# Two mixture-of-experts layers on one core: the routed experts' loop staged by quads of slot tiles instead of pairs

## The chip, the cores and the metric

The kernel runs on one core of a Trainium2 chip. A core has five engines, each with an instruction stream of its own that is worked off in order: TensorE (PE in the profile, its weight loads PEld), VectorE (DVE), ScalarE (ACT), GpSimd (POOL) and SyncE (SP). They meet through semaphores only. PE reads SBUF and writes PSUM (eight banks of 512 float32 a partition); DVE and ACT take results out of PSUM. DMAs are issued from the streams of SP and ACT, and indirect ones (a row index for each row) from POOL's.

The metric is the device time of one execution in microseconds; the time of a kernel is the median of its runs.

## What is computed

The input is x of 4 x 1024 tokens with 256 channels, all float32. Two layers, each `x = x + s * silu(ffn(xn))` with `xn` the layer norm of x and `s` a mixer of `xn`: in layer 0 a gated linear recurrence over the 1024 steps, in layer 1 an attention over cosines. The part that matters here is the ffn, a mixture of 16 experts of which each token takes 4, chosen by group-limited top-k. In layer 0:

```python
g = jnp.einsum('th,eih->tei', x, gate_proj)
u = jnp.einsum('th,eih->tei', x, up_proj)
act = jax.nn.silu(g) * u
expert_out = jnp.einsum('tei,ehi->teh', act, down_proj)
y = jnp.einsum('teh,te->th', expert_out, combine)
```

Layer 1 has the same form with a shared expert of 512 hidden channels added. An expert's hidden width is 128 in layer 0 and 64 in layer 1.

## The kernel before

Tokens are sorted by expert. A router gives each of a token's four choices a *slot*; the token's row is scattered to `rows_in` in DRAM by indirect DMA on POOL (line 587). Slots are cut into tiles of 128 rows, every tile belongs to one expert, and four tiles make a quad. Each layer has two groups of tokens and 160 tiles in all, which is 80 pairs or 40 quads. `experts` (from line 592) is a generator that both layers use; `w_sb` holds all experts' weights, and a register that PE loads from `of_tile` (line 480, eight tiles at a time) says where a tile's expert begins.

For a pair of tiles the generator has four steps:

- `turn` (lines 635 and 639): the rows `xs` of a quad come by one DMA (line 626, three quads ahead, on SP in layer 0 and mostly on ACT in layer 1); PE transposes two tiles by two halves of 128 channels into a bank `tp`, and ACT copies it to `xT`.
- `hidden` (line 647, then 473, 474 and 658): PE multiplies `xT` by gate and up weights into a bank `gu` (64 x 2 or 128 x 2 columns a tile, so in layer 1 half the bank is left free); ACT makes tanh, DVE two steps, and the result is `h`.
- `turn_hidden` (lines 664 and 666): PE transposes the two tiles of `h` into a bank `tp`, ACT copies them to `hT`. In layer 1 a transposed tile has 64 partitions.
- `down` (line 672): PE multiplies `hT` by the down weights into a bank `acc`. The first pair of a quad is copied to `o` by DVE (line 690), the second by ACT (line 684); then the quad is stored, in layer 0 by one DMA on ACT's queue (line 723), in layer 1 by four indirect DMAs on POOL (line 1212).

The steps are pipelined by pairs. Round j of the loop issues `turn` of pair j+2, `hidden` of j+1, `turn_hidden` of j and `down` of j-1, with a `yield` after each. Two copies of a bank and four of `xT`/`h` (tag `act`) and `sg`/`hT` (tag `sg`) are there.

The yields set what is mixed in. `run` counts a planned clock on by 0.81 (layer 0) or 0.64 us (layer 1) a yield, and lets other generators, `Beside`, issue their pieces when they are due: in layer 0 the last recurrence, the combine of finished groups (gathers on POOL, line 730) and layer 1's routing; in layer 1 preparation of the last batch for the attention (line 1013), and the final combine, `gated1` (line 1250). The tile framework then orders each engine's stream by its own estimate; what is listed below as a program's order is the built one. After layer 0's experts come attention and shared expert for three batches beside the combine, then the dispatch of layer 1 (128 scatters), layer 1's experts, and the last batch's shared expert and attention.

Of the kernel before, what the change touches and what calls it, by code (L numbers as in the profile page):

```python
# [9 lines left out]
F32 = mybir.dt.float32  # L10
# [6 lines left out]
P = 128  # L17
B, S, D = 4, 1024, 256
# [5 lines left out]
XB, GB, QB, OB = 8, 4, 3, 3  # L24
# [6 lines left out]
QUAD = 4  # L31
# [32 lines left out]
def two_layer_kernel(  # L64
# [18 lines left out]
    nc = tc.nc  # L83
# [3 lines left out]
    work = ctx.enter_context(tc.tile_pool(name="work", bufs=2))  # L87
# [5 lines left out]
    def bank(tag, bufs):  # L93
        tag = side[0] if tag == "side" else tag
        return psum.tile([P, 512], F32, tag=tag, name=tag, bufs=bufs)
# [42 lines left out]
    ident = const.tile([P, P], F32, tag="ident", name="ident")  # L138
# [3 lines left out]
    for n in (G, E):  # L142
        m = const.tile([P, max(2 * NT, *(len(h) * NS for h in HALVES)), n], F32, tag=f"run{n}", name=f"run{n}")
# [43 lines left out]
    def latest(engine):  # L187
        return next(i for i in reversed(nc.cur_bb.bb.instructions) if i.engine == engine)
# [282 lines left out]
    def twice_silu(dst, t, v):  # L471

        nc.scalar.activation(t, v, AF.Tanh, scale=0.5)  # L473
        nc.vector.scalar_tensor_tensor(dst, t, 1.0, v, ALU.add, ALU.mult)  # L474

    def offset(table, engine, u, cache, most):

        if u not in cache:
            n = min(8, table.shape[1] - u)
            _, values = nc.values_load_multi_w_load_instructions(  # L480
                table[0:1, u : u + n],
                engines=[engine],
                min_val=0,
                max_val=most,
                skip_runtime_bounds_check_because="the kernel holds it to the last expert's",
            )
            for i, v in enumerate(values):
                cache[u + i] = v
        return cache[u]
# [14 lines left out]
    def by_quads(rows):  # L504

        return rows.rearrange("(n p i) d -> n p i d", p=P, i=QUAD)
# [94 lines left out]
    def experts(groups, of_tiles, w_sb, we, hid, store, target=None, begin=None, end=None):  # L601

        per = QUAD // 2
        quads = [(i, g, q) for i, g in enumerate(groups) for q in range(NSLOT[g] // QUAD)]
        n = len(quads) * per
        width = rows_in[groups[0]].shape[1]
        offsets, loaded, made, targets = [{} for _ in groups], {}, {}, {}  # L610

        def expert(t):
            i, _, q = quads[t // QUAD]
            return offset(of_tiles(i), mybir.EngineType.PE, q * QUAD + t % QUAD, offsets[i], (E - 1) * we)

        def load(at):
            if at >= len(quads):
                return
            _, g, q = quads[at]
            if q == 0 and begin:  # L620
                begin(g)
            xs = work.tile([P, QUAD, D + INFO], F32, tag="q", name="xs", bufs=QB)
            xs = xs.rearrange("p i d -> p (i d)")[:, 0 : QUAD * width].rearrange("p (i d) -> p i d", d=width)

            engine = nc.scalar if g >= G1 and at > 2 else nc.sync
            engine.dma_start(out=xs, in_=by_quads(rows_in[g])[q])
            loaded[at] = xs

        def turn(j):
            xs = loaded[j // per]  # L630
            tp = bank("tp", 2)
            for i in range(2):
                for kc in range(KC):
                    at = (i * KC + kc) * P
                    nc.tensor.transpose(  # L635
                        tp[:, at : at + P], xs[:, j % per * 2 + i, kc * P : (kc + 1) * P], ident
                    )
            xT = work.tile([P, 2, KC, P], F32, tag="act", name="xT", bufs=4)
            nc.scalar.copy(xT.rearrange("p i k t -> p (i k t)"), tp)  # L639
            return xT  # L640

        def hidden(j, xT):
            ps = bank("gu", 2)[:, 0 : 4 * hid]
            for i in range(2):
                off = expert(2 * j + i)
                for kc in range(KC):
                    nc.tensor.matmul(  # L647
                        ps[:, i * 2 * hid : (i + 1) * 2 * hid],
                        lhsT=xT[:, i, kc, :],
                        rhs=w_sb[:, bass.ds(off + kc * 2 * hid, 2 * hid)],  # L650
                        start=(kc == 0),
                        stop=(kc == KC - 1),
                    )
            gu = ps.rearrange("p (i w h) -> p i w h", i=2, w=2)
            sg = work.tile([P, 2, hid], F32, tag="sg", name="sg0", bufs=4)
            h = work.tile([P, 2, hid], F32, tag="act", name="h0", bufs=4)
            twice_silu(h, sg, gu[:, :, 0, :])
            nc.vector.tensor_tensor(h, h, gu[:, :, 1, :], ALU.mult)
            return h

        def turn_hidden(h):
            tp = bank("tp", 2)
            for i in range(2):
                nc.tensor.transpose(tp[0:hid, i * P : (i + 1) * P], h[:, i, :], ident)  # L664
            hT = work.tile([P, 2 * P], F32, tag="sg", name="hT0", bufs=4)
            nc.scalar.copy(hT[0:hid, :], tp[0:hid, 0 : 2 * P])  # L666
            return hT

        def down(j, hT):
            ps = bank("acc", 2)  # L670
            for i in range(2):
                nc.tensor.matmul(  # L672
                    ps[:, i * D : (i + 1) * D],
                    lhsT=hT[0:hid, i * P : (i + 1) * P],
                    rhs=w_sb[0:hid, bass.ds(expert(2 * j + i) + 4 * hid, D)],
                    start=True,
                    stop=True,
                )
            if j % per == 0:
                made[j // per] = work.tile([P, QUAD, D], F32, tag="o", name="o", bufs=OB)  # L680
            o = made[j // per]
            to = o[:, j % per * 2 : j % per * 2 + 2, :].rearrange("p i d -> p (i d)")
            if j % per == per - 1:
                nc.scalar.copy(to, ps)
                _, g, q = quads[j // per]
                store(g, q, made.pop(j // per), targets.pop(j // per, None))
                if end and q == NSLOT[g] // QUAD - 1:
                    end(g)
            else:
                nc.vector.tensor_copy(to, ps)  # L690

        xT, h, hT = {}, {}, {}
        load(0)
        load(1)
        load(2)
        yield
        for j in range(-2, n + 1):
            if j + 2 < n:
                at, last = divmod(j + 2, per)
                if last and target:  # L700

                    with tc.issue_after(latest(mybir.EngineType.DVE)):
                        targets[at] = target(quads[at][2], loaded[at])
                xT[j + 2] = turn(j + 2)
                if last:
                    loaded.pop(at)
                    load(at + 3)
            yield
            if 0 <= j + 1 < n:
                h[j + 1] = hidden(j + 1, xT.pop(j + 1))  # L710
            yield
            if 0 <= j < n:
                hT[j] = turn_hidden(h.pop(j))
            yield
            if 0 <= j - 1:
                down(j - 1, hT.pop(j - 1))
            yield

    def experts0():


        def store(g, q, o, _):
            nc.scalar.dma_start(out=by_quads(rows_out[g])[q], in_=o)

        return experts(range(G1), lambda i: routed[i][1], w0_sb, WE, P, store, end=stored.add)
# [460 lines left out]
    def experts1():  # L1186
# [35 lines left out]
        def end(g):  # L1222
            stored1[g - G1] = max(clock[0], pool_free[0]) + LANDING

        return experts(range(G1, 2 * G1), lambda i: placed1[i][2], we1_sb, WE1, P // 2, store, target, begin, end)

    def gated1(b):
# [250 lines left out]
```

## Time and profile before

| what | value |
|---|---|
| median of 4 runs (lowest, highest) | 1443.6 us (1440.87, 1448.89) |
| the profiled execution's own time | 1447.49 us |
| its span, first to last instruction | 1445.8 us |
| mean granted clock of TensorE | 0.861 of full |
| busy: PE, PEld, DVE, ACT, POOL | 1084.8, 796.0, 648.2, 461.6, 559.1 us |
| gates, line 647: 1280 matmul records | 248.0 us busy |
| down, line 672: 640 records | 188.2 us busy |
| row transposes, line 635: 640 | 105.4 us busy |
| transposes of `h`, line 664: 320 | 64.1 us busy |
| result stores, line 1212: 160 | 159.9 us busy |

A float32 matmul stands in the trace as two records, a transpose as one. Matmuls are pipelined: the duration of a record covers its way through the array, and the next starts earlier than it ends, so the cost of one in a stream is the step from start to start. `PEclk` is the share of full clock that PE was granted. "issue" as the end of an idle time means that the profile shows nothing the engine waited for.

### The profile page before, as it was taken

The page shows a single profiled execution, that of the slowest core. Times are in us where ns is not written, and L with a number is a line of the kernel's source. Part 1 is how long each engine was busy: PE and PEld are TensorE (multiplying, and loading weights), DVE is VectorE, ACT ScalarE, POOL GpSimd, SP SyncE. Part 2 cuts the span into 40 slices and gives each one's busy share as a digit, 9 for nine tenths or more (in the row PEclk, how much of TensorE's full clock was granted, in tenths as well). Part 3 has the DMA queues.
Part 4 walks back from the last instruction along what each step waited for, and adds up shares of the span by engine and source line. Part 5 has one row for each costly group of instructions (what it writes and reads, how often), then busy time and mean ns, then how long its engine had stood idle before and what let it go on. Part 6 is the DMA issues. An engine that isn't in the chain of part 4 may idle for free.

```text
span 1445.8 us, 16114 instructions
## 1 busy us (share of the span) xinstructions
PE 1084.8 (75%) x4928; PEld 796.0 (55%) x4928; DVE 648.2 (45%) x1928; ACT 461.6 (32%) x1028; POOL 559.1 (39%) x589
## 2 busy tenths in 40 slices
PE   6427671399938989938688934625999998999997
PEld 4214351288837778726356712314767676666566
DVE  4903930033227863125976714200235333567485
ACT  3503440144314544302222400001226443454322
POOL 0470377400254000254332775771004665566300
PEclk9756895599969999957889976857999999899999
DMA  9983254377958668765235624320113555896681
GB/s 347 415 325 88 88 160 158 120 210 218 263 169 289 196 168 228 288 163 168 81 108 184 209 104 152 132 104 37 73 66 130 174 169 185 286 318 228 200 271 56
DMA packets 118994, 264.81 MB, mean 183 GB/s; under 512 B 14208, under 2 KB 71680, under 8 KB 117632
## 3 DMA queue, kind: packets, MB, share of 16 engines
q1 hardware_dynamic: 78256, 138.79, 30.8%
q0 software_dynamic: 27264, 75.86, 15.5%
q10 hardware_dynamic: 13392, 49.14, 9.6%
q8 instruction: 43, 0.70, 0.2%
q14 instruction: 39, 0.32, 0.1%
HBM read 119.34 MB, written 144.39 MB: 182 GB/s over the span
## 4 chain that ended last, share of the span: by engine, by line
PE 55%; another core or an unknown queue 18%; DVE 16%; issue 6%; ACT 3%; DMA 1%; POOL 0%; ACTq 0%; DVEq 0%; POOLq 0%
PE gu L647 13%; PE acc L672 10%; PE tp L635 5%; PE acc L1098 5%; PE gu L1145 4%; PE tp L664 3%; PE acc L1161 3%; PE mm L1145 3%; PE mm L1066 2%; PE gu L1013 1%; DVE stats L197 1%; PE acc L301 1%; DVE hT L545 1%; PE mm L519 1%
## 5 line engine op out<-in xcount | busy, mean ns | idle before, releaser
L730 POOL DMA_INDIRECT r<-rows_out,row x128 | 128.4, 1003 | 368.8 <-issue 172.8
L647 PE MATMUL gu<-w_sb,xT 128*128 x1280 | 248.0, 338 | 4.0 <-issue 3.0
L1212 POOL DMA_INDIRECT results<-o,dest x160 | 159.9, 1000 | 213.4 <-DVE h L474 129.7
L647 PEld LDWEIGHTS gu<-w_sb,xT 128*128 128x128 f32 x1280 | 201.6, 199 | 20.0 <-issue 5.0
L672 PE MATMUL acc<-w_sb,hT 128*128 (+1 forms) x640 | 188.2, 411 | 8.0 <-ACT hT L666 8.0
L587 POOL DMA_INDIRECT rows_in<-x_half,row x128 | 132.1, 1032 | 137.1 <-issue 88.4
L474 DVE SCALAR_TENSOR_TENSOR h<-sg,gu 128x256 f32<-128x256 f32 (+1 forms) x160 | 56.1, 351 | 261.5 <-ACT sg L473 196.3
L1098 PE MATMUL acc<-val,es 128*128 128x256 f32 x512 | 132.6, 402 | 27.0 <-ACT es L1078 25.1
L587 POOL DMA_INDIRECT rows_in<-t_half,row x128 | 125.9, 984 | 39.4 <-issue 37.0
L635 PE MATMUL tp<-ident,xs 128*128 128x128 f32 x640 | 105.4, 289 | 41.8 <-ACT xT L639 21.6
L672 PEld LDWEIGHTS acc<-w_sb,hT 128*128 128x128 f32 (+1 forms) x640 | 111.6, 196 | 38.0 <-issue 16.8
L639 ACT COPY xT<-tp 128x512 f32<-128x512 f32 x160 | 93.8, 587 | 112.3 <-PE tp L635 49.8
L1098 PEld LDWEIGHTS acc<-val,es 128*128 128x128 f32 x512 | 99.3, 202 | 52.4 <-ACT es L1078 27.1
L635 PEld LDWEIGHTS tp<-ident,xs 128*128 128x128 f32 x640 | 76.7, 146 | 78.0 <-issue 40.3
L473 ACT ACTIVATE sg<-gu 128x256 f32<-128x256 f32 (+1 forms) x160 | 53.1, 332 | 185.0 <-PE gu L647 107.9
L664 PE MATMUL tp<-ident,h 128*128 128x128 f32 (+1 forms) x320 | 64.1, 283 | 62.0 <-issue 31.0
L1161 PE MATMUL acc<-w_sb,act 128*128 128x256 f32 x256 | 67.4, 413 | 56.6 <-DVE act L1155 29.5
L690 DVE COPY o<-acc 128x512 f32<-128x512 f32 x80 | 55.1, 689 | 93.0 <-PE acc L672 47.4
L1161 PEld LDWEIGHTS acc<-w_sb,act 128*128 128x128 f32 x256 | 52.3, 207 | 77.6 <-issue 35.2
L664 PEld LDWEIGHTS tp<-ident,h 128*128 128x128 f32 (+1 forms) x320 | 37.7, 129 | 84.9 <-issue 52.3
L1145 PE MATMUL gu<-xnT,w_sb 128*128 128x512 f32 x128 | 65.8, 638 | 23.9 <-issue 17.8
L1066 PE MATMUL mm<-projT 128*128 128x512 f32 (+3 forms) x192 | 71.9, 498 | 0.0
(225 smaller groups left out, 1496.5 us busy)
## 6 DMA issues: line engine op xcount, KB each, us to landing
rows_in<-zeros SPq DMA_DIRECT2D x20, 1044.0 KB
xs<-rows_in SPq DMA_DIRECT2D x40, 512.0 KB
rows_out<-o ACTq DMA_DIRECT2D x40, 512.0 KB
xs<-rows_in ACTq DMA_DIRECT2D x37, 522.0 KB
r<-results SPq DMA_DIRECT2D x32, 512.0 KB
rows_in<-zeros SPq DMA_DIRECT2D x1, 12288.0 KB
rows_in<-zeros SPq DMA_DIRECT2D x1, 8192.0 KB
w_sb<-in_w_dram SPq DMA_DIRECT2D x4, 1536.0 KB
```

What stands on the lines that cost most here:

```text
L587: nc.gpsimd.indirect_dma_start(out=view, out_offset=bass.IndirectOffsetOnAxis(ap=row[:, c0 + s, k : k + 1], axis=0), in_=tokens[:, s, :], ...
L635: nc.tensor.transpose(tp[:, at : at + P], xs[:, j % per * 2 + i, kc * P : (kc + 1) * P], ident)
L639: nc.scalar.copy(xT.rearrange("p i k t -> p (i k t)"), tp)
L647: nc.tensor.matmul(ps[:, i * 2 * hid : (i + 1) * 2 * hid], lhsT=xT[:, i, kc, :], rhs=w_sb[:, bass.ds(off + kc * 2 * hid, 2 * hid)], start= ...
L664: nc.tensor.transpose(tp[0:hid, i * P : (i + 1) * P], h[:, i, :], ident)
L672: nc.tensor.matmul(ps[:, i * D : (i + 1) * D], lhsT=hT[0:hid, i * P : (i + 1) * P], rhs=w_sb[0:hid, bass.ds(expert(2 * j + i) + 4 * hid, D ...
L730: nc.gpsimd.indirect_dma_start(out=r[:, k, :], out_offset=None, in_=rows_out[g], in_offset=bass.IndirectOffsetOnAxis(ap=row[:, c, k : k + ...
L1066: nc.tensor.matmul(ps[:, at:TB], lhsT=projT[kc][:, t * P : (t + 1) * P], rhs=projT[kc][:, q * TB + at : (q + 1) * TB], start=(kc == 0), st ...
L1098: nc.tensor.matmul(av[s // 2][:, (s % 2) * D : (s % 2 + 1) * D], lhsT=es[:, s * P : (s + 1) * P], rhs=val[t // NS][:, t % NS, :], start=(t ...
L1145: nc.tensor.matmul(ps, lhsT=w[:, kc, j * P : (j + 1) * P], rhs=xr[:, kc, :], start=(kc == 0), stop=(kc == KC - 1),)
L1161: nc.tensor.matmul(ys[s // 2][:, (s % 2) * D : (s % 2 + 1) * D], lhsT=h[:, s * P : (s + 1) * P], rhs=ds1_sb[:, j, :], start=(j == 0 and s ...
L1212: nc.gpsimd.indirect_dma_start(out=views[g - G1][QUAD * q + i], out_offset=bass.IndirectOffsetOnAxis(ap=dest[:, i : i + 1], axis=0), in_=o ...
```

## The change

Both layers' experts run in stages of a quad. Round m issues the gates of quad m (8 matmuls), the row transposes of quad m+1 (8), the down products of quad m-1 (4) and the transposes of quad m's activations (4). In layer 1 the gates of four tiles fill one `gu` bank (`span` is 2; in layer 0 it is 1, a bank a pair), so tanh and the two DVE steps work on 256 elements at once; the four transposed activations of a quad share a `tp` bank and one copy. A round has eight yields, as two rounds of before had, and there is one round more than half of before.

```diff
-        def hidden(j, xT):
-            ps = bank("gu", 2)[:, 0 : 4 * hid]
+        def hidden(m, j, xT):
+            if j % span == 0:
+                gates[m] = bank("gu", 2)
+            ps = gates[m][:, 0 : 4 * span * hid]
+            at = j % span * 2
...
+            if j % span < span - 1:
+                return
+            gu = ps.rearrange("p (i w h) -> p i w h", i=2 * span, w=2)
+            sg = work.tile([P, 2 * span, hid], F32, tag="sg", name="sg0", bufs=4)
+            h = work.tile([P, 2 * span, hid], F32, tag="act", name="h0", bufs=4)
             twice_silu(h, sg, gu[:, :, 0, :])
             nc.vector.tensor_tensor(h, h, gu[:, :, 1, :], ALU.mult)
-            return h
+            hs_of.setdefault(m, []).extend(h[:, i, :] for i in range(2 * span))
-        def turn_hidden(h):
+        def turn_hidden(m):
             tp = bank("tp", 2)
-            for i in range(2):
-                nc.tensor.transpose(tp[0:hid, i * P : (i + 1) * P], h[:, i, :], ident)
-            hT = work.tile([P, 2 * P], F32, tag="sg", name="hT0", bufs=4)
-            nc.scalar.copy(hT[0:hid, :], tp[0:hid, 0 : 2 * P])
+            for i, h in enumerate(hs_of.pop(m)):
+                nc.tensor.transpose(tp[0:hid, i * P : (i + 1) * P], h, ident)
+            hT = work.tile([P, QUAD * P], F32, tag="sg", name="hT0", bufs=4)
+            nc.scalar.copy(hT[0:hid, :], tp[0:hid, :])
             return hT
...
-        for j in range(-2, n + 1):
-            if j + 2 < n:
...
-                xT[j + 2] = turn(j + 2)
-                if last:
-                    loaded.pop(at)
-                    load(at + 3)
-            yield
-            if 0 <= j + 1 < n:
-                h[j + 1] = hidden(j + 1, xT.pop(j + 1))
-            yield
-            if 0 <= j < n:
-                hT[j] = turn_hidden(h.pop(j))
-            yield
-            if 0 <= j - 1:
-                down(j - 1, hT.pop(j - 1))
-            yield
+        span = 512 // (4 * hid)
+        for m in range(-1, len(quads) + 1):
+            for j in range(per):
+                if 0 <= m < len(quads):
+                    hidden(m, j, xT.pop((m, j)))
+                yield
+            for j in range(per):
+                if m + 1 < len(quads):
...
+                    xT[m + 1, j] = turn((m + 1) * per + j)
+                    if j == per - 1:
+                        loaded.pop(m + 1)
+                        load(m + 4)
+                yield
+            for j in range(per):
+                if 0 <= m - 1:
+                    down(m - 1, j, hT[m - 1])
+                yield
+            hT.pop(m - 1, None)
+            if 0 <= m < len(quads):
+                hT[m] = turn_hidden(m)
+            yield
+            yield
```

## The prediction

> **What bounds the kernel now.** I read three views in this order: where TensorE (PE) has free time in each stage, what one step of the expert loop costs on PE, and what else works beside it.
>
> First the table of busy time by stage (us from the span's start; busy time of PE, PEld, DVE, ACT, POOL; the granted clock; DMA).
>
> ```profile
> 282.00:395.00 113.00, 111.09 (x604) 96.37 (x604) 38.71 (x85) 50.78 (x120) 7.78 (x9) 0.98 0.80 230
> 395.00:430.00 35.00, 12.12 (x40) 9.22 (x41) 5.94 (x14) 4.90 (x11) 20.36 (x22) 0.66 0.56 164
> 430.00:525.00 95.00, 82.23 (x427) 68.69 (x426) 76.59 (x237) 45.37 (x93) 18.31 (x19) 0.95 0.75 228
> 525.00:590.00 65.00, 65.00 (x350) 55.55 (x350) 21.24 (x46) 31.07 (x74) 0.00 (x0) 1.00 0.70 190
> 600.00:1000.00 400.00, 250.35 (x870) 169.89 (x869) 170.72 (x569) 75.16 (x169) 217.06 (x232) 0.77 0.44 143
> 1000.00:1078.00 78.00, 77.88 (x297) 52.97 (x295) 21.48 (x44) 17.41 (x48) 0.00 (x0) 1.00 0.13 48
> 1078.00:1250.00 172.00, 157.92 (x966) 119.82 (x966) 68.34 (x232) 81.82 (x188) 95.05 (x98) 0.98 0.55 183
> 1250.00:1346.00 96.00, 87.19 (x492) 64.35 (x492) 68.99 (x188) 44.36 (x108) 57.72 (x55) 0.91 0.75 254
> ```
>
> Layer 0's experts run from 187 to 590, layer 1's from 1078 to 1346. PE is full from 282 to 395, from 525 to 590 and from 1000 on, and the end of the span hangs on PE's last products; so a microsecond saved on PE after 1078 should come off the end. PE starves only where POOL issues indirect DMAs without a pause (395 to 430 here, and 205 to 282).
>
> Second, PE's own timeline, one pair of slot tiles in layer 0 and one in layer 1 (start, duration, line, tiles; a duration is modelled and overlaps the next start, so I read starts).
>
> ```profile
> 344.47 0.60 PE L635 MATMUL tp<-ident,xs 128*128 128x128 f32 x4
> 344.91 1.89 PE L647 MATMUL gu<-w_sb,xT 128*128 x8
> 346.64 0.38 PE L664 MATMUL tp<-ident,h 128*128 128x128 f32 x2
> 346.86 1.03 PE L672 MATMUL acc<-w_sb,hT 128*128 x4
> 347.72 0.60 PE L635 MATMUL tp<-ident,xs 128*128 128x128 f32 x4
> ```
>
> ```profile
> 1183.40 0.66 PE L635 MATMUL tp<-ident,xs 128*128 128x128 f32 x4
> 1183.90 1.06 PE L647 MATMUL gu<-w_sb,xT 128*128 x8
> 1184.79 0.38 PE L664 MATMUL tp<-ident,h 128*64 128x128 f32 x2
> 1185.10 1.13 PE L672 MATMUL acc<-w_sb,hT 64*128 x4
> 1186.16 0.66 PE L635 MATMUL tp<-ident,xs 128*128 128x128 f32 x4
> ```
>
> From start to start, layer 0's pair takes 0.44 (row transposes) + 1.73 (gates) + 0.22 (transposes of the activations) + 0.86 (down) = 3.25 us. Four transposes in 0.44 and eight matmul records in 1.73 are the steps of 0.109 and 0.216 us that these instructions keep inside their groups: nothing is lost where one kind follows another. Layer 1's pair takes 0.50 + 0.89 + 0.31 + 1.06 = 2.76. Its gates are half as wide (0.89), the other three have the shapes of layer 0 in time, and yet are 0.06, 0.09 and 0.20 longer: **0.35 us a pair** is lost around the down products, whose weights have 64 rows (64*128) between neighbours of 128 rows.
>
> Third, what else runs in layer 1: the page's POOL line of the result stores, and the DVE groups.
>
> ```profile
> L1212 POOL DMA_INDIRECT results<-o,dest x160 | 159.9, 1000 | 213.4 <-DVE h L474 129.7 <-issue 39.7 <-ACT o L684 14.6
> L690 DVE COPY o<-acc 128x512 f32<-128x512 f32 x80 | 55.1, 689 | 93.0 <-PE acc L672 47.4 <-issue 16.9 <-DMA results<-o,dest 10.8
> ```
>
> Four stores of a quad start 1.27 us apart (1182.08, 1183.35, 1184.61, 1185.88), 5.1 us a quad; layer 1 takes 267/40 = 6.7 us a quad, so POOL is not the bound, but not far from it.
>
> **Layer 1's sum before.** 80 pairs without the loss: 80 x 2.41 = 193, and 32 records of the value product at 0.216 = 7: 200 us. In the built program's order the down products come in 101 runs and not in 80, since 44 of them are cut to one tile around a transpose: 101 x 0.35 = 35. The stretch is 267, so 32 us are waits: some twenty of 0.5 to 2.5 us before lines 664, 672 and 635, mostly at the end of a run of six or more stores on POOL, when PE's results are seen late by ACT.
>
> **The change, part by part.** Each round still issues every matmul, transpose, weight load, register load and DMA of before; a quad has 8 gate, 8 row-transpose, 4 down and 4 activation-transpose products in that order. In the built program layer 1's down products are 40 runs of four.
>
> (a) *Layer 1's switches to 64 rows and back.* 40 in place of 101: 61 x 0.35 = **-21 us**, all on PE, where PE is the bound. Bounds: 0, if the loss belongs to each down pair and not to the switch (against that: inside a run the steps are 0.216 except the second, 0.320); -27, if the waits around the 44 split runs go too.
>
> (b) *Layer 0's switches.* Its timeline shows none that costs, so **0**, although half the changes of kind go.
>
> (c) *ACT and DVE.* Layer 1: one tanh and one pair of DVE steps over 256 elements for two over 128. Layer 0's rows of that width are 0.386, 0.419 and 0.417 us, layer 1's 0.278, 0.284 and 0.286, so a quad saves 0.17 on ACT and 0.30 on DVE; one hT copy of 512 (0.587, as xT) replaces two of 256 (0.37): 0.15. Some 18 us of ACT and 12 of DVE, **0** here: both sit beside PE (82 of 172 and 68 of 172 us busy). If the cover goes, they are a gain.
>
> (d) *The new waits.* Behind a waiting PE instruction the whole quad queues. The transposes of the activations wait for tanh and two DVE steps: 0.39 + 0.42 + 0.42 and about 0.3 between engines, 1.5 us. Ahead of them stood another pair's transposes, down, row transposes and gates: 0.22 + 0.86 + 0.44 + 1.73 = 3.25 in layer 0 and 2.7 in layer 1. Now stand 8 row transposes and 4 downs: 0.87 + 1.73 = 2.6 in layer 0, 2.8 in layer 1. Cover is left, 1.1 us instead of 1.7 in layer 0. It goes where DVE has other work queued (430 to 525 and 1250 to 1346, with steps of 0.48 to 1.23 us ahead): 15 + 15 quads. Cost between 0 and 1.2 us each, 0 to 36 us in all; in the old order the same stretches show waits of some 10 us each, once per pair; halved in number and somewhat longer I take **+4 us**. Gates wait for xT: two copies of 0.59 against 1.73 + 0.43 of PE, covered. Downs wait for hT: 0.6 against gates and row transposes, covered.
>
> (e) *Queues.* Row loads keep their place behind the last row transpose of a quad and three quads ahead, on SP and ACT. On SP two loads for the combine now stand ahead of layer 1's weights (before: behind); SP waits there 24.6 us for layer 0's last down anyway, so **0**; 3 us (2 x 512 KB at 300 GB/s) if their buffers are late. POOL's order is unchanged.
>
> (f) *Depth.* A quad's down comes a whole quad after its gates, so the last quad ends with a bare hT copy: 0.6 us a layer, **+1**.
>
> (g) *600 to 1078.* Nothing is edited, but the builder's order of attention, shared expert and routing shifts by a few instructions, in a stretch where PE is starved by POOL. Bounds -10 to +10, taken as **0**.
>
> Sum: -21 + 4 + 1 = -16 us. The profiled execution took 1447.5 us (its span 1445.8), 3.9 over the median 1443.6 of the four runs: 1447.5 - 16 = 1431.5 there, and **1428 us** for a median.
>
> A rule against it. In the trace weight loads of 0.19 us run beside the matmuls before them, all rows alike, at steps of 0.216, and the load is uncovered only where the number of rows changes. The Trainium skill ("TensorE: Matmul & The Clock Gate", Part 3, "What overlaps and what doesn't") says that a weight load overlaps a running matmul only when its row group differs. By that rule same-row neighbours would be the costly ones and (a) would be nothing or a loss: about 1448. The rows decide.
>
> **Rivals.**
> 1. *POOL holds PE.* With 5.3 us of PE a quad against 5.1 of POOL, stores run without a pause, and unbroken runs are what starves PE at 395 to 430. If the stretch stays at 6.4 us a quad, the gain is 0.3 x 40 = 12; at 6.6 it is 4: 1436 to 1447, say **1440**. For it: the waits at the ends of long runs. Against: a run of twelve stores (1118 to 1134) passed without a wait.
> 2. *Slower: the wait on h.* If the transposes wait 1.2 us a quad in the DVE-loaded stretches, +36 against -21 gives about **1459**; it decides from 21/30 = 0.7 us a quad. For it: DVE at 77 of 95 us busy. Against: DVE works in order and its h steps are half as many in layer 1.
> 3. *More gain.* In the starved stretches (205 to 282, 395 to 430) PE moves one step for each result that gets through; with two pairs a step it could go some 4 pairs further, 4 x 3.25 = 13: **1413**.
> 4. *Not what it says*: a builder that splits the stages again. The built order has 40 runs of four in layer 1 and 39 in layer 0, so nearly excluded.
>
> **How the numbers follow.** Forecast 0.48 (1428, 1420 to 1436), rival 1 0.17, rival 2 0.18, rival 3 0.15, rival 4 0.02. About 0.5% (7 us) is what a measurement here tells from no change. Faster by more: the forecast, rival 3 and a little of rival 1: 0.64. Within: most of rival 1, rival 4 and the near end of rival 2: 0.19. Slower: 0.17. The range takes in rival 3's 1413 with (g)'s 8 below it, and rival 2 to 1456: 1405 to 1456.
>
> **What would show it.** After: 1078 to 1346 shrinks to about 250; PE's layer-1 quad goes at steps of 0.89 x 2, 0.87, 0.3 + 1.73, 0.43; weight loads of line 672 lose most of their idle time "issue". Layer 0's full stretches keep 6.5 us a quad. Wrong would be: quads of 6.5 in layer 1 with POOL without pauses (rival 1), PE waiting for DVE's h at the transposes of the activations (rival 2), or a shift between 200 and 1078 larger than that of layer 1.

## The result

After: 1455.9 us, the median of 37 runs (1435.6 to 1471.1), beside 1448.6 us before (58 runs, 1432.0 to 1467.2). The ratio is **1.0041** (95% interval 1.0019 to 1.0063). The forecast was 1428, faster; what was measured is a small loss, inside the 0.5% that I called no change, and opposite in sign to the forecast. Ratios, here and below, leave out runs over 1.5% above the fastest one of the same kernel, so they are not the quotients of the medians beside them. The profiled execution of after took 1446.8 us (span 1445.1).

Later runs fell under two conditions that nobody chose: beside some the kernel before took 1446 to 1463 us, as here, and beside others 1125 to 1127. I call them **H** and **F** (the expectations below speak of a chip of the second kind, or with the hold, for H, and of the first kind, or without it, for F), and compare only with before beside the same runs. In what is compared below, the cause looked for is there under H and not under F.

### The profile page after: what moved, and what is told of

Same layout as the page of the kernel before. It is cut to its first block, busy times and chain, and to the rows that moved or that the text cites. A ratio compares the mean times of both kernels' runs of the same rounds, so it can differ in the third digit from the quotient of the medians.

```text
span 1445.1 us, 15677 instructions
## 1 busy us (share of the span) xinstructions
PE 1081.6 (75%) x4928; PEld 821.0 (57%) x4928; DVE 641.4 (44%) x1848; ACT 448.8 (31%) x908; POOL 557.8 (39%) x589
## 4 chain that ended last, share of the span: by engine, by line
PE 49%; another core or an unknown queue 22%; DVE 16%; issue 5%; ACT 4%; DMA 2%; POOL 1%; ACTq 0%; DVEq 0%; POOLq 0%
PE gu L650 12%; PE acc L678 7%; PE acc L1109 6%; PE tp L634 3%; PE mm L1077 3%; PE tp L669 3%; PE mm L1156 2%; PE gu L1156 2%; PE acc L1172 2%; DVE stats L197 1%; PE acc L301 1%; PE gu L1024 1%; DVE x_half L1261 1%; DVE y L808 1%
## 5 line engine op out<-in xcount | busy, mean ns | idle before, releaser
L650 PEld LDWEIGHTS gu<-w_sb,xT 128*128 128x128 f32 x1280 | 214.4, 212 | 33.1 <-issue 12.0
L474 DVE SCALAR_TENSOR_TENSOR h<-sg,gu 128x256 f32<-128x256 f32 x120 | 50.3, 419 | 329.9 <-ACT sg L473 229.5
L678 PE MATMUL acc<-w_sb,hT 128*128 (+1 forms) x640 | 163.4, 396 | 16.5 <-issue 16.5
L678 PEld LDWEIGHTS acc<-w_sb,hT 128*128 128x128 f32 (+1 forms) x640 | 118.2, 194 | 40.3 <-issue 23.9
L634 PE MATMUL tp<-ident,xs 128*128 128x128 f32 x640 | 88.8, 278 | 39.2 <-issue 39.1
L473 ACT ACTIVATE sg<-gu 128x256 f32<-128x256 f32 x120 | 45.9, 384 | 222.6 <-PE gu L650 114.5
L669 PE MATMUL tp<-ident,h 128*128 128x128 f32 (+1 forms) x320 | 55.2, 298 | 59.6 <-ACT xT L638 28.3
L638 ACT COPY xT<-tp 128x512 f32<-128x512 f32 x160 | 87.4, 589 | 23.3 <-remote 8.0
L669 PEld LDWEIGHTS tp<-ident,h 128*128 128x128 f32 (+1 forms) x320 | 36.4, 135 | 83.1 <-ACT xT L638 52.6
L690 ACT COPY o<-acc 128x512 f32<-128x512 f32 x80 | 47.1, 589 | 107.7 <-PE acc L678 50.8
L1156 PE MATMUL mm<-xnT,w_sb 128*128 128x512 f32 x128 | 64.1, 624 | 16.9 <-DVE act L474 16.9
```

What stands on the lines that cost most here:

```text
L634: nc.tensor.transpose(tp[:, at : at + P], xs[:, j % per * 2 + i, kc * P : (kc + 1) * P], ident)
L650: nc.tensor.matmul(ps[:, (at + i) * 2 * hid : (at + i + 1) * 2 * hid], lhsT=xT[:, i, kc, :], rhs=w_sb[:, bass.ds(off + kc * 2 * hid, 2 * h ...
L669: nc.tensor.transpose(tp[0:hid, i * P : (i + 1) * P], h, ident)
L678: nc.tensor.matmul(ps[:, i * D : (i + 1) * D], lhsT=hT[0:hid, at * P : (at + 1) * P], rhs=w_sb[0:hid, bass.ds(expert(m * QUAD + at) + 4 * ...
L1156: nc.tensor.matmul(ps, lhsT=w[:, kc, j * P : (j + 1) * P], rhs=xr[:, kc, :], start=(kc == 0), stop=(kc == KC - 1),)
```

## The profile after

Two rows of the table by stage, of after (stretch, busy PE, PEld, DVE, ACT, POOL, granted clock, DMA), answer to the last two of before:

```profile
1078.00:1250.00 172.00, 146.10 (x901) 125.07 (x900) 57.20 (x166) 68.52 (x129) 93.43 (x96) 0.91 0.52 173
1250.00:1346.00 96.00, 81.44 (x496) 69.47 (x496) 64.03 (x160) 38.96 (x76) 54.36 (x54) 0.87 0.74 250
```

PE issues no more there than before (901 records against 966, 496 against 492), is less busy, and its granted clock fell from 0.98 to 0.91 and from 0.91 to 0.87. So it waits more, and it works slower after waiting. Taken by the code, from layer 1's first row transposes to its last down product, the stretch grew from 273.1 to 281.2 us. Layer 0 did not change: 406 us before, 408 after.

PE's timeline of after, first a quad that nothing holds up:

```profile
1156.00 1.95 PE L650 MATMUL gu<-w_sb,xT 128*128 x16
1157.79 1.04 PE L634 MATMUL tp<-ident,xs 128*128 128x128 f32 x8
1158.75 1.99 PE L678 MATMUL acc<-w_sb,hT 64*128 x8
1160.67 0.63 PE L669 MATMUL tp<-ident,h 128*64 128x128 f32 x4
1161.14 1.95 PE L650 MATMUL gu<-w_sb,xT 128*128 x16
```

Gates to gates are 1.79 + 0.96 + 1.92 + 0.47 = 5.14 us, against two pairs of 2.76 before: 0.38 us a quad are saved, as step (a) has it. Then one that is held up:

```profile
1129.37 1.99 PE L678 MATMUL acc<-w_sb,hT 64*128 x8
1135.30 1.03 PE L669 MATMUL tp<-ident,h 128*64 128x128 f32 x4 [3.95 <-DVE xs L1205]
1136.13 3.19 PE L650 MATMUL gu<-w_sb,xT 128*128 x16
1139.16 1.04 PE L634 MATMUL tp<-ident,xs 128*128 128x128 f32 x8
```

The transposes of `h` waited 3.95 us, and the gates behind them took 3.03 us from start to start where the quad above took 1.79: from 1135.4 to 1138.7 the granted clock was 0.50, half. The gates at 1149.47 took 3.17 us, behind a single wait of 1.50, and there too the granted clock was 0.50 (1149.0 to 1152.3). By the Trainium skill ("TensorE: Matmul & The Clock Gate", Part 1) an idle window of about 3.4 us sends the clock to half. The first wait agrees with that, the second is shorter than such a window, and half clock followed it in this trace all the same.

Where does such a wait come from? The timeline of after, all engines, around another one:

```profile
1181.47 1.95 PE L650 MATMUL gu<-w_sb,xT 128*128 x16
...
1183.22 0.59 ACT L690 COPY o<-acc 128x512 f32<-128x512 f32 x1 [3.00 <-remote]
...
1184.08 0.96 POOL L1223 DMA_INDIRECT results<-o,dest  x1 [0.55 <-issue]
1184.67 0.58 ACT L671 COPY hT<-tp 64x512 f32<-64x512 f32 x1 [0.87 <-PE tp L634]
...
1185.34 0.96 POOL L1223 DMA_INDIRECT results<-o,dest  x1 [0.30 <-issue]
...
1187.59 0.38 ACT L473 ACTIVATE sg<-gu 128x256 f32<-128x256 f32 x1 [2.34 <-PE acc L678]
...
1188.01 0.42 DVE L474 SCALAR_TENSOR_TENSOR h<-sg,gu 128x256 f32<-128x256 f32 x1 [6.98 <-ACT sg L473]
1188.46 0.42 DVE L663 TENSOR_TENSOR h<-h,gu 128x256 f32<-128x256 f32 x1
...
1189.03 0.60 PE L669 MATMUL tp<-ident,h 128*64 128x128 f32 x4 [1.14 <-DVE xs L1205]
```

PE's gates end at 1183.4. ACT's tanh of them, which needs nothing else, starts at 1187.59, **4.2 us later**, having stood idle for 2.34 us before it (the profile names the last of PE's instructions that it sees, not the one that was needed). ACT works in order, and the two copies ahead of tanh were late as well: that of `acc` by 2.1 us, that of `hT` by 0.87. From 1176.1 POOL issued eight stores with pauses of at most 0.55 us; the last ended at 1186.30, and 1.3 us after it ACT went on. At nine of the eleven runs of eight tanh starts 1.1 to 1.7 us after the run's end: at 1119.60 after the run that ended at 1118.0, at 1133.87 after 1132.2, at 1167.25 after 1166.0. So PE's results are *held* while POOL issues stores one after the other. Not all are held to the end of a run. Those of its first microseconds pass (tanh at 1123.46, in the run begun at 1122.39, followed its gates by 0.04 us), and some copies start inside a run, like that of `hT` at 1184.67 here and at 1128.14, 1.0 to 1.1 us after the end of a store's row.

```profile
L1223 POOL DMA_INDIRECT results<-o,dest x160 | 158.1, 988 | 229.2 <-ACT o L690 117.6 <-DVE o L696 61.2 <-issue 39.9
L684 ACT COPY o<-acc 128x512 f32<-128x512 f32 x80 | 46.9, 587 | 41.8 <-PE acc L672 25.3 <-remote 9.1 <-DMA results<-o,dest 1.9
L690 ACT COPY o<-acc 128x512 f32<-128x512 f32 x80 | 47.1, 589 | 107.7 <-PE acc L678 50.8 <-remote 26.0 <-PE tp L669 11.8
```

The first is the group of stores in after: they cost the same (988 ns against 1000), but before they ran mostly by twos, fours and sixes, with two runs of eight and a last one of twelve, and after in 11 runs of eight, 15 of four and a last one of twelve (pauses up to 0.6 us counted as none). The other two are ACT's copies of a quad's second pair, before and after, in both layers together: they waited 9.1 us, then 26.0, for "remote", a releaser that the profile cannot find on this core. On the page of before, 18% of the chain of waits was "another core or an unknown queue", on that of after 22%. This share is of the whole program and tells little of layer 1: it was 17% in a later profile of after under H, and 19% with plain stores.

## The experiments

**Theory A**: PE's quad got shorter (5.1 us for 5.5) and so as short as POOL's four stores (5.07); the stores of two quads then join to an unbroken run, PE's results are held for its length, and waits and half clock eat the gain. **Theory B**: staging by quads makes PE wait by itself, for tanh, DVE and the copies. **Theory C**: the loss lies in layer 0 or between the layers.

All results in one table. "Stretch" is layer 1 from its first row transposes to its last down product in the profiled run; "waits" is what PE's steps there, from start to start, last beyond their usual length, where that is over 0.25 us; steps that half clock makes longer stay under that, one by one, and are not in it. (A second profile of before under H: 272.7 and 29.4.)

| kernel | before beside it | time | ratio (95%) | stretch | waits |
|---|---|---|---|---|---|
| before, H | | 1448.6 | 1 | 273.1 | 32.8 |
| after, H | 1448.6 | 1455.9 | 1.0041 (1.0019 to 1.0063) | 281.2 | 48.9 |
| after again, H | 1448.2 | 1461.9 | 1.0144 (1.0077 to 1.0211) | 278.6 | 45.3 |
| layer 1 alone by quads, H | 1446.3 | 1455.3 | 1.0042 (1.0001 to 1.0083) | 282.4 | 43.8 |
| layer 0 alone by quads, H | 1446.3 | 1450.6 | 1.0018 (0.9986 to 1.0051) | 273.0 | 32.9 |
| before, plain store, H | 1446.3 | 1430.6 | 0.9861 (0.9776 to 0.9946) | 250.4 | 13.7 |
| after, plain store, H | 1446.3 | 1419.0 | 0.9783 (0.9709 to 0.9858) | 239.0 | 17.7 |
| after, plain store, POOL busy, H | 1462.6 | 1428.0 | 0.9796 (0.9721 to 0.9871) | 239.4 | 17.7 |
| after, three copies, H | 1448.2 | 1435.1 | 0.9952 (0.9916 to 0.9987) | 253.9 | 29.7 |
| after, one copy, H | 1462.6 | 1469.1 | 1.0049 (1.0005 to 1.0094) | 277.7 | 42.5 |
| before, stores put off, H | 1448.2 | 1447.0 | 0.9989 (0.9938 to 1.0040) | 278.2 | 36.4 |
| before, by eight, H | 1462.6 | 1497.0 | 1.0268 (1.0193 to 1.0342) | 316.0 | 60.7 |
| **after, F** | 1126.5 | 1107.0 | **0.9836** (0.9812 to 0.9859) | 224.6 | 9.8 |
| before, stores put off, F | 1127.4 | 1126.6 | 1.0007 (0.9980 to 1.0033) | 245.2 | 10.0 |
| after, plain store, POOL busy, F | 1127.4 | 1121.6 | 0.9941 (0.9909 to 0.9974) | 239.4 | 17.3 |
| after, three copies, F | 1127.4 | 1142.6 | 1.0144 (1.0120 to 1.0168) | 254.2 | 27.5 |
| after, two copies, F | 1125.5 | 1125.4 | 1.0000 (0.9983 to 1.0017) | 239.2 | 20.7 |
| before, three copies, F (twice) | 1127.4, 1125.5 | 1138.1, 1136.6 | 1.0107, 1.0099 | 253.2, 253.4 | 16.5, 17.3 |

### Without the stores on POOL

```diff
-            for i in range(QUAD):
-                nc.gpsimd.indirect_dma_start(out=views[g - G1][QUAD * q + i], ...)
+            rows = results[g - G1][q * QUAD * P : (q + 1) * QUAD * P]
+            nc.sync.dma_start(out=rows.rearrange("(i p) d -> p i d", p=P), in_=o)
```

In after:

> The kernel after, with layer 1's result rows stored in slot order by one plain DMA a quad on SP in place of four indirect DMAs on POOL (so the rows do not reach their tokens' places; left out is only the scatter). Theory A (PE's quad is shorter, 5.1 us in place of 5.5, but POOL's stores, 5.07 us a quad, then run unbroken by eights, and PE's results reach ACT only after such a run): without POOL's stores the long waits go, layer 1's experts run at 5.1 to 5.4 us a quad, their stretch falls from 279 to some 210 us and the whole to about 1390; and it beats the pair version with the same plain stores by 8 to 20 us. Theory B (the quad staging itself makes PE wait, for tanh, DVE and the copies): the waits before the transposes and downs stay, 6.0 us a quad or more, and it is no faster than the pair version with plain stores.

In before:

> The kernel before, with the same plain store of layer 1's result rows. Theory A: pairs at 5.5 us a quad, the stretch 271 falls to some 225, the whole to about 1403, 8 to 20 us slower than the quad version with plain stores. Theory B: as fast as the quad version or faster.

Measured: both lose more than half of their waits, and the order turns round: quads 239.0 us, pairs 250.4, and 1419.0 against 1430.6 (the intervals of the two ratios overlap; each is clear of 1). Mechanism as A has it, size short of it: 239 in place of 210 for the quads, 250 in place of 225 for the pairs. From 1123 to 1226 each quad takes 5.14 us from gates to gates, but the fourteen from there to 1313 take 6.2; PE waits 8.4 us in all for DVE's `h`, 7.3 of them after 1200, as DVE's stream stands still for rows of the final combine (once for 2.75 us, at 1255). That is the prediction's rival 2, and with 17.7 against 13.7 it is worth the +4 us of step (d).

### One layer at a time

`experts` takes the old body for one layer and the new one for the other:

```diff
+        return by_pairs() if hid == P else by_quads_()
```

(the condition turned round for the second kernel).

> Layer 0's experts staged by pairs as before, layer 1's by quads as after. Theory A: layer 1's stretch is some 8 us longer than before's 271 us (279), with stores by eights on POOL; the time stands 5 to 12 us above before. Theory C (the loss comes from layer 0 or from the work between the layers): layer 1's stretch is as in before or shorter, and the time is that of before or lower.

> Layer 0's experts by quads as after, layer 1's by pairs as before. Theory A: layer 1's stretch 271 us as before; layer 0 ends at the same time, and what layer 1's start gained in the kernel after (9 us earlier) is kept to the end, so 3 to 9 us below before if that shift comes with layer 0's edit, no difference if it does not. Theory C: slower than before by 7 us or more.

Measured: the loss comes with layer 1's edit (1.0042; stretch 282.4), and layer 0's gives nothing that can be told (1.0018, an interval that holds 1; layer 1's stretch 273.0). C falls. The 9 us by which layer 1 began earlier in after's profile belong to neither: over these H profiles it begins between 1068 and 1091, in before's own two at 1076.8 and 1091.1.

### Breaking the runs

Three copies on POOL, 0.36 us each, ahead of a quad's stores (two and one in the later kernels):

```diff
         def store(g, q, o, dest):
             indirect(QUAD)
+            for k in range(3):
+                nc.gpsimd.tensor_copy(scratch[:, k * D : (k + 1) * D], o[:, QUAD - 1, :])
```

The first runs of these kernels fell under F, where before takes 1127:

> The kernel after, with three small copies on POOL (128x256, some 1.3 us together by POOL's rows of copies and memsets, an estimate) ahead of a quad's four result stores, into columns that nothing reads; nothing is left out. POOL has more to do, 6.4 us a quad, and its runs of stores are cut at four. Theory A, by length of run: results of PE are held only until a run of stores ends, so the waits of PE in layer 1 fall from 49 us to 20 to 28, the stretch from 281 to some 260, the whole to 1430 to 1440: faster for more work on POOL. Theory A', by number of stores however spaced (their transfers or descriptors slow the others): the waits stay at 49, and the stretch grows to 281 or more, the whole to 1456 to 1475.

> The kernel before with the same three copies on POOL ahead of a quad's stores. Theory A: before's runs of six and eight are cut at four, its waits of 33 us fall to some 25 and the stretch to 263 to 270; the whole 1436 to 1446. Theory A': 273 or more, 1446 to 1465.

There both were slower, by 1.4 and 1.1%: there was no hold to break, and POOL's 6.03 us a quad became the bound (stretch 254 and 253). A forecast for H, so it tells nothing for or against A. Under H:

> The kernel after with three copies of 128x256 on POOL ahead of a quad's stores, as in the run of that name. On a chip of the second kind (before 1446): theory A, by length of run: PE's waits fall from 49 to 20 to 28 us, the stretch from 281 to some 260, the whole to 1430 to 1440; theory A', by number of stores: waits of 49 or more, 1456 to 1475. On a chip of the first kind there is no hold to break, and POOL's 6.1 us a quad is the bound: 1140, slower than before by 1 to 2%.

Measured: **1435.1 where after beside it took 1461.9**, and 0.9952 of before: faster than both kernels, although POOL has 40 x 1.1 us more to do. The stretch is 253.9, waits 29.7, and A' falls. Its timeline (POOL's stores and copies, ACT's tanh):

```profile
1181.36 0.96 POOL L1225 DMA_INDIRECT results<-o,dest  x1 [0.31 <-issue]
...
1182.33 1.08 POOL L1222 COPY w_sb<-o 128x256 f32<-128x256 f32 x3
1183.35 0.38 ACT L473 ACTIVATE sg<-gu 128x256 f32<-128x256 f32 x1 [2.78 <-PE acc L678]
1183.57 0.98 POOL L1225 DMA_INDIRECT results<-o,dest  x1 [0.17 <-issue]
```

Here tanh starts 1.03 us after the last store's row ended (1182.32), and in the next quad 1.04 us after (1189.40, 1188.36), each time just before the next store. So even four stores hold PE's results, but a release a quad is enough. The same kernel has this stretch under F (254.2): with the runs broken, the condition no longer matters there. How short may the break be?

> The kernel after with one copy of 128x256 on POOL ahead of a quad's stores instead of three. The copies took 0.36 us each, so the break is 0.5 us between two stores and POOL asks 5.3 us a quad instead of 6.03. If any instruction that is not an indirect DMA lets the held results through: waits near 35 us or less, the stretch 235 to 250, the whole 1415 to 1432, the fastest of all. If the break must be longer (about 1.2 us passed between the end of a run and the release in the kernel after): waits of 45 or more, stretch 270 to 281, 1447 to 1460.

Measured: 0.5 us does not do: 277.7, waits 42.5, 1.0049. Its tanh at 1146.78 stood 5.2 us idle, through a break from 1142.75 to 1143.32. It agrees with the 1.03 us above.

> The kernel after with two copies of 128x256 on POOL ahead of a quad's stores: a break of 0.9 us between two stores where one copy (0.5 us) did not let PE's results through and three (1.25 us) did; POOL asks 5.65 us a quad. If 0.9 us is long enough: waits near 35 us or less, stretch 240 to 254, 0.985 to 0.995 of before. If not: runs that act like those of eight, waits of 43 or more, stretch 272 to 281, 1.000 to 1.010 of before. On a chip without the hold (before 1127): POOL's 5.65 us a quad is the bound, 0 to 1% slower than before.

This run (0.9 us) and the second of before with copies fell under F, so whether 0.9 us is enough under H, and whether breaks help pairs as much as quads there, stays open:

> The kernel before with three copies on POOL ahead of a quad's stores, as in the run of that name, for a chip of the second kind. POOL asks 6.03 us a quad, 241 us for 40, against PE's 5.5. If the quads of the kernel after are worth their 0.4 us only where POOL leaves room, both kernels with three copies are bound by POOL alike: stretch 253 to 258 as in after_pause_2 (254), 0.993 to 0.999 of before. If pairs are worse off with pauses too: stretch 262 to 270, 1.000 of before or above.

### Is it POOL's being busy?

After with the plain store of above, and POOL filled with memsets:

```diff
+            nc.gpsimd.tensor_copy(scratch[:, 0:16], o[:, QUAD - 1, 0:16])
+            for _ in range(5):
+                nc.gpsimd.memset(scratch[:, 0:1024], 0.0)
```

> The kernel after with the plain store by SP (no scatter, rows stay in slot order), and POOL kept busy instead by five memsets of 128x1024 and a small copy that waits for the quad's result, 0.94 x 5 + 0.24 = 4.95 us a quad. If a busy POOL holds PE's results, whatever it does, the waits are those of the kernel after (49 us) and the time 1450 or so. If only the issue of indirect DMAs does, it is as with the plain store alone: waits of 18 us, 1419 plus or minus 6.

> The kernel after with plain stores by SP and POOL kept busy by memsets, 4.95 us a quad, as in the run of that name, for a chip of the second kind (before 1446 to 1449). If any busy POOL holds PE's results: waits of some 45 us and a time of 1450. If only the issue of indirect DMAs does: waits of 18 us, a stretch of some 239, 0.978 of before as with the plain store alone, 1413 to 1425.

The first run fell under F (0.9941, 239.4). Under H: 0.9796, waits 17.7 and stretch 239.4, those of the plain store alone. The timeline of this H run:

```profile
1180.17 1.95 PE L650 MATMUL gu<-w_sb,xT 128*128 x16
...
1181.23 0.95 POOL L1229 MEMSET w_sb<- 128x1024 f32 x1
...
1182.16 0.38 ACT L473 ACTIVATE sg<-gu 128x256 f32<-128x256 f32 x1 [1.21 <-PE gu L650]
```

Tanh starts with the end of the gates (1182.12), in the middle of unbroken work on POOL. Memsets that keep POOL as busy as the stores do not hold PE's results.

### Long runs with PE's old order

The first attempt put off the call of a quad's stores until the next quad's:

> The kernel before, with layer 1's result stores put off so that two quads' eight stores are issued together (a fourth result buffer in columns that nothing reads). PE's order is that of before, by pairs. Theory A: the runs of stores are of eight as in after, PE's waits in the stretch grow from 33 to 45 us or more and the stretch from 273 to 283 or more; the whole 1456 or more. Theory B (the staging by quads is what waits): stretch and time as in before, 1442 to 1450.

> The kernel before with layer 1's stores issued by eights, as in the run of that name. On a chip of the second kind: theory A, waits of 45 us or more and a stretch of 283 or more in place of 33 and 273, the whole 1456 or more; theory B, as before, 1442 to 1450. On a chip of the first kind no difference from before.

It made no eights under H: POOL's stream has the same order either way, and the first four stores waited for nothing new; the runs stayed at two to six, with three longer ones. So 0.9989 says nothing on A or B. (Under F POOL merely fell behind, and with its runs of 8 to 16 PE's waits were 10.0 us.) The second one ties the first quad's row numbers to the second quad's result:

```diff
+            nc.vector.scalar_tensor_tensor(first, o[:, QUAD - 1, 0:QUAD], 0.0, held[0][3], ALU.mult, ALU.add)
+            held[0] = (*held[0][:3], first)
```

> The kernel before, with layer 1's stores issued for two quads at a time, and the row numbers of the first quad made to hang on the second quad's results (one more DVE step of 128x4 for two quads), so that its stores cannot start earlier. PE's order is by pairs as in before. Theory A: runs of eight, 10 us long, every two quads; PE's waits in layer 1 grow from 28 to 33 us to 45 or more and the stretch from 273 to 283 or more, the whole to 1456 or more. Theory B (the staging by quads is what waits): 273 and 1442 to 1452. Where the chip shows no hold (before 1127): within 1% of before.

Measured: 1.0268, waits 60.7, stretch 316.0, with runs of six and eight. Around the end of one run of eight:

```profile
1179.03 1.06 PE L647 MATMUL gu<-w_sb,xT 128*128 x8
...
1183.12 0.96 POOL L1224 DMA_INDIRECT results<-w_sb,dest  x1 [0.30 <-issue]
...
1183.69 1.97 PE L647 MATMUL gu<-w_sb,xT 128*128 x8
1185.76 0.28 ACT L473 ACTIVATE sg<-gu 128x128 f32<-128x128 f32 x1 [3.02 <-PE gu L647]
```

The gates of 1179.03 end at 1180.1 and their tanh starts at 1185.76, 5.7 us later and 1.7 after the run's last store (one copy to `xT`, ahead of tanh in ACT's order, was let through at 1182.16). The pairs' order is held just as the quads' is; B is not needed for it, though the loss is larger than A said, and the edit's own delay of the stores is in it.

### After where nothing is held

> The kernel after itself, once more. Four runs with the kernel before at 1127 us beside them showed a chip on which runs of eight, sixteen and forty-eight stores, scatters or gathers pass on POOL and no result of PE is held; on the other chip before takes 1446 to 1449. Theory A (the hold takes the gain): on a chip of the first kind, before at 1127, after is faster, by 8 to 18 us (the 11.6 us between the two kernels with plain stores up to the 15 us of PE's shorter quads); on a chip of the second kind 1.000 to 1.008 of before as measured. Theory B (the staging by quads makes PE wait, whatever POOL does): not faster on either.

> The kernel before, for its profile beside the others of this call. On a chip of the first kind: no idle time put down to another core or an unknown queue, and layer 1's stretch near 235 to 245 us; of the second kind: 18% of the chain put down to that, and 273 us.

These fell under H: 1.0144, more than the 1.008 at most that A had given, and for before a single run, of 1461.7, with a stretch of 272.7. The last run fell under F:

> The kernel after itself. On a chip without the hold (before near 1126): theory A, 0.984 to 0.993 of before, since PE's quad is 0.4 us shorter and nothing holds its results, with POOL's 5.07 us a quad just below PE's 5.1; theory B, 0.998 or more. On a chip with the hold (before 1446 to 1463): 1.002 to 1.015.

Measured: **0.9836** (0.9812 to 0.9859), 19.4 us faster. The chain of waits on the page of this run, and then its timeline:

```profile
PE 70%; DVE 18%; DMA 4%; issue 3%; ACT 2%; POOL 2%; DVEq 0%; ACTq 0%; POOLq 0%
```

```profile
870.42 0.96 POOL L1223 DMA_INDIRECT results<-o,dest  x1 [0.30 <-issue]
...
871.20 1.04 PE L634 MATMUL tp<-ident,xs 128*128 128x128 f32 x8
871.40 0.38 ACT L473 ACTIVATE sg<-gu 128x256 f32<-128x256 f32 x1 [1.21 <-PE gu L650]
871.69 0.96 POOL L1223 DMA_INDIRECT results<-o,dest  x1 [0.30 <-issue]
...
876.34 0.93 PE L634 MATMUL tp<-ident,xs 128*128 128x128 f32 x7
```

"Another core or an unknown queue" is gone from the chain. POOL issues 88 stores with no pause over 0.65 us (822.9 to 935.9), tanh starts at once (the gates end at 871.36), and a quad takes 5.14 us (871.20 to 876.34). Theory A's condition is met, and its gain is there.

## Why the prediction was wrong

- **(a), -21 us: right.** Under F the stretch is 20.6 us shorter than that of the pairs (245.2, of the put-off kernel, which equals before in time there), and the whole 19.4. Under H the unheld quad is 5.14 for 5.52.
- **(b), (c), (e): right.** Layer 0 took 406 and 408 us, and its edit alone changes nothing; no run shows ACT's and DVE's savings come off the end. (f), +1, was not measured by itself.
- **(g): right within its bounds.** The start of layer 1 moves by some 20 us between profiles, with no tie to the edit.
- **(d), +4 us: the step that failed.** Where nothing is held, +4 is about what the plain stores show (17.7 for 13.7). Under H the waits grew by 16.1 us (32.8 to 48.9), and most of them stand behind a tanh or a copy that started late, which (d) did not count: it had DVE's queue alone. The clock lost, by the rows by stage, 0.07 x 172 + 0.04 x 96 = 16 us more, an estimate from above since it counts idle time too; counted on PE's own steps while the granted clock was half, it is 8.2 us before and 19.9 after, 12 more. Sum: -20.6 + 16.1 + 12 = +7.5, measured +8.1. The clock had no term in my sum at all.
- **"PE is full from 1000 on"**, on which the step from PE's work to the end of the span rested, was misread: the same table has PE busy for 157.92 of 172 us and for 87.19 of 96 after 1078.
- **Rival 1 was the case, at a wrong price and a wrong chance.** I had seen that runs without a pause starve PE at 395 to 430, but let the result rest on "POOL is not the bound", which compares sums: 5.1 us a quad against 6.7. The cost does not lie in POOL's share but in how long its stores run without a break. With PE's quad brought down to 5.14, beside 5.07 of stores, there are eleven runs of eight where before had two. I priced that at 4 to 12 us of gain left; none was left. My evidence against it, twelve stores from 1118 to 1134 without a wait, was misread: they stood in groups of two and four with breaks of 0.7 to 0.9 us.
- **Not more lateness, but longer pieces of it.** In layer 1's traces I counted the starts of tanh and of ACT's copies to `xT` and `hT` that came over 0.4 us after both PE's product and ACT's work before were done. Before has 41, together 57 us, the longest 3.8; after has 24, together 54 us, the longest 5.2. (In the later H profiles it is 50 and 55 us by pairs, 62 and 53 by quads; with plain stores 5 and 6.5, in after under F 2.) So the edit added little lateness or none; it gathered it, and PE waited 48.9 us for it in place of 32.8. Part of that is the longer runs, which cost pairs dear too (before by eight: 81 us late, waits 60.7). Part may be the quads' order, in which a whole quad queues behind a waiting instruction. No run separates the two.
- **Rivals 2, 3, 4** were not the case; 2 shows only in the plain-store kernels, and is small there.

Not settled: what holds the results, and why not under F. The Trainium skill ("Perfetto Trace Analysis", DMA Instruction — SWDGE (GPSIMD)) says that the profiler's end of such a DMA is when its descriptors are written, not when its data has moved. So the 1.03 us behind the last row may be the transfers'; no run here tests it, and the trace's DMA packets do not decide it: the last of POOL's queue before the tanh of 1187.59 in after ended at 1187.39, but with three copies ten of them were still under way when the tanh of 1183.35 started. Nor was it tried to break the dispatch's and the gathers' runs of 16 to 80, though much of the 320 us between H and F lies beside them: layer 0's experts alone take 406 us under H and 306 under F.

## What to carry to other kernels

An engine that is "not the bound" by its share can still set the pace by the shape of its work: ask how long its runs last and which engines wait meanwhile, above all when another engine's period is brought down to meet its own. A sign in the profile is a consumer that starts microseconds after its producer's end, with "remote" or a long finished instruction as releaser; look what ends at that moment on the other engines. And price a wait together with the clock that is lost behind it.

## What the runs showed of the hardware

- Under H, some of PE's results reach ACT late in a run of indirect DMAs on POOL, by up to 5.2 us, the last of them 1.0 to 1.7 us after the run's end (after, eleven runs of eight). A break of 0.5 us in the run did not release them, breaks of 1.25 us did. Memsets that kept POOL busy for 4.95 us a quad did not hold them (waits 17.7 us, as without).
- Under F, 88 stores in a row held none of these results, and the kernel before takes 1126 instead of 1448 us. Durations of the instructions are the same (stores 0.96, gates 1.95 us a quad in both). The chips numbered 1 and 12 in the runs' records appear under both, so the condition does not follow the chip's number.
- Adding work can pay: 44 us of copies on POOL made the kernel 27 us faster than after, and 0.5% faster than before, under H; under F the same copies cost 36 us against after.
